# One written order from the end of attention to the cross softmax, PSUM banks handed back one by one

## The chip, the cores and the metric

The kernel runs on one core of one Trainium2 chip. The time is device microseconds of one execution. The engines are named as in the profile: PE (TensorE, the matmuls) with its weight loads PEld, DVE (VectorE), ACT (ScalarE), POOL (GpSimd) and SP (SyncE, here the queue that issues DMAs). PE writes to PSUM, which has eight banks of 128 x 512 f32; everything else lies in SBUF.

## The reference

One decoder layer over x (8 sequences of 128 tokens, width 512) and a context of the same shape, each of three parts added to x and followed by a layer norm:

```python
x = _layernorm(x + attn(x))        # 32 heads on 8 key heads, 4-bit weights, rope, causal softmax
x = _layernorm(x + xattn(x, ctx))  # 16 heads of 32
x = _layernorm(x + ffn(x))         # gated low-rank experts
```

The cross attention has an unusual softmax: it runs over the *batch and heads* (axis 0 of the scores), not over the keys:

```python
scores = jnp.einsum('bqd,bkd->bqk', Q, K) / sqrt(32)      # b = 8 sequences x 16 heads
attn = jax.nn.softmax(scores, axis=0)
```

So for each pair of positions there are 128 scores to be normalised together, and no cross output can be formed before the scores of all sequences and heads are there.

## The kernel before, in words

**Order.** From the first projection on, the instructions of PE, DVE, ACT and POOL are in an order written out by hand: each engine runs its instructions in the order in which the program issues them (`tc.manual_schedule(engines=ORDERED)`, line 700), and waits for data, for a free buffer or a free bank where it has to. `later(n, f)` (line 236) puts an operation off by n slots, and `tick()` issues what has come due.

**Attention** is a loop of 64 steps (line 745), eight sequences for each of the eight key heads; each step issues the letters of `SEQUENCE`. After every fourth step, 16 output units are queued (`attention_out`, line 436): the product of the attention result with the output weights, four column blocks c by four heads r. A unit "O" is two matmuls into the bank of one of two lanes (`out0`, `out1`); between heads the partial sum in the bank is multiplied by a ratio of scales, and after the fourth head it is added to `accT`. A unit therefore waits for the rescaling of the unit before it in its lane. The rescaling is made by ACT (line 456), or by DVE while the flag `ending` is set (line 454), which is from step 58 to step 63.

**The end of attention** (line 826, `ATT_END`) issues the last 16 O, mixed with 14 units "K" of the context's keys (three matmuls each, four to a bank, `x_projection`) and eight "X" (`turn_out`, line 816): four transposes of `accT`, the residual added to `acc` by DVE, and the layer norm's statistics by DVE, its power by POOL (line 222). The norm is applied later, by two ACT instructions, `nmr` and the scaling (lines 227 and 228). Then the pools of attention are closed, in SBUF and in PSUM.

**The cross softmax** (line 845 on). The query weights are loaded in four pieces and each is split into a high part (ACT, line 176) and a low part (POOL, line 177). `turn_x1` (line 881) transposes a normed sequence; ACT copies it as the high part and DVE makes the low part. `queries(r)` makes one block of queries, with 12 matmuls (line 679). `products(r)` makes the scores of group r (32 small matmuls into four banks, line 930). There are eight groups of 16 (sequence, head) pairs. A round of the loop at line 992 is: `exponentials(r)`, in which DVE subtracts the running maximum from each bank (line 954) and ACT takes the exponential; `products(r + 1)`; `queries(r + 3)`; `group_maximum(r + 1)`, five DVE instructions (lines 943 to 948); some of the 32 units of the context's values (`work`, the list `fill`); `group_sum(r)` on POOL (line 962). After the last round a sum over everything is made by PE with the identity (line 1042), then DVE's reciprocal (line 1089). All eight banks turn in a circle under one name here.

**The cross values and the FFN** (line 1324 on). For each sequence: `cross_values` (PE, line 1254), the residual, statistics, norm (`normalised` again, for the tokens "x" and for the gates "g"), transposes, the gate's and the main products. The first sequence's iteration also issues the last four value units.

Of the kernel before, what the change touches and what calls it, by code (L numbers as in the profile page):

```python
# [19 lines left out]
P = 128  # L20
# [22 lines left out]
ATT_END = 'OOKXOOKXOOKXOOKXOOKOOKOOKOOKKXKXKXKXKK'  # L43
# [9 lines left out]
FIRST_FILL = 4  # L53
ROUND_FILL = (0, 4, 4, 0, 4, 4, 4)
SUM_FILL = 4
# [65 lines left out]
BANKS_FIRST = {"turn": 6, "out0": 1, "out1": 1}  # L121
BANKS_SECOND = {"turn": 8}
BANKS = {m: 1 for m in ("pa", "pb", "pc", "pd", "sc", "tr", "av", "po")}
# [7 lines left out]
def decoder_kernel(ctx: ExitStack, tc: tile.TileContext, a: dict, out: bass.AP):  # L131
# [4 lines left out]

    psum = {"n": BANKS_FIRST, "turn": 0, "cm": tc.tile_pool(name="banks", bufs=1, space=PSUM)}
    psum["pool"] = psum["cm"].__enter__()

    def bank(tag, name, shape=(P, 512)):  # L140
        if tag == "proj" and "pa" in psum["n"]:
            tag = "p" + "abcd"[psum["turn"] % 4]
            psum["turn"] += 1
        tag = tag if tag in psum["n"] else "turn"
        return psum["pool"].tile(list(shape), F32, tag=tag, name=name, bufs=psum["n"][tag])
# [68 lines left out]
    def normalised(x, name):  # L214

        st = stat.tile([P, 6], F32, tag="bn", name=f"bn_{name}")
        nc.vector.bn_stats(st[:], x)
        mv = stat.tile([P, 2], F32, tag="mv", name=f"mv_{name}")
        nc.vector.bn_aggr(mv[:], st[:])
        rstd = stat.tile([P, 1], F32, tag="rstd", name=f"rstd_{name}")  # L220
        nc.vector.tensor_scalar(rstd[:], mv[:, 1:2], EPS, None, ALU.add)
        nc.gpsimd.tensor_tensor(rstd[:], rstd[:], minus_half[:], ALU.pow)
        nmr = stat.tile([P, 1], F32, tag="nmr", name=f"nmr_{name}")
        nc.vector.tensor_scalar(mv[:, 0:1], mv[:, 0:1], -1.0, None, ALU.mult)

        def apply():
            nc.scalar.activation(nmr[:], mv[:, 0:1], AF.Copy, scale=rstd[:])
            nc.scalar.activation(x, x, AF.Identity, scale=rstd[:], bias=nmr[:])

        return apply  # L230
# [34 lines left out]

    att_cm, att = pool("att")
# [95 lines left out]
    def projections(g, hf, w):  # L362

        n = f"{g}_{hf}"
        q = att.tile([P, REP, HN], F32, tag="q", name=f"q{n}", bufs=2)
# [48 lines left out]
    def attention_values(g, b, t, pt):  # L414
# [3 lines left out]
        if j == 0:  # L418
            for m in "hl":
                t["c" + m] = att.tile([P, REP, HN], F32R, tag="c" + m, name=f"c{m}{n}", bufs=2)  # L420
# [49 lines left out]
    def new_o(g):  # L470
# [6 lines left out]
        att.tile([P, KT, HN], F32, tag=tag, name=f"xraw{hf}", bufs=2) for hf, tag in enumerate(("q", "wo"))  # L477
# [13 lines left out]
    w0_q = att.tile([P, REP, D], F32R, tag="ch", name="w0_q", bufs=2)  # L491
# [87 lines left out]
    def open_keys():  # L579
# [4 lines left out]
        raw = xk["ctx0"] = att.tile([P, KT, HN], F32, tag="q", name="ctxraw0", bufs=2)  # L584
        nc.sync.dma_start(raw[:], a["ctxT"].rearrange("(k p) n -> p k n", p=P)[:, :, ts(0, HN)])

    def open_cross():
# [47 lines left out]
        def vals(t, tag="proj"):  # L635
# [4 lines left out]
            def part(kt):  # L640
                if kt == 0:
                    bk.append(bank(tag, f"pxv{t}"))
# [4 lines left out]
                if kt == KT - 1:  # L647
                    nc.tensor.matmul(bk[0][:], both[:], bias[:], start=False, stop=True)
                    nc.scalar.copy(values_of(t), bk[0][:])

# [12 lines left out]
    def values_of(t):  # L663

        hf, j = divmod(t, HALF)
        if len(xk["v"]) == hf:
            pl, tag = ((e2, "v"), (xk["work"], "ch0"))[hf]
# [3 lines left out]
    def x_projection(dst, m, w, x, hf, o, tag="proj"):  # L671
        bk = []

        def part(kt):
            if kt == 0:
                bk.append(bank(tag, f"px{m}{hf}_{o}"))
# [9 lines left out]
            if kt == KT - 1:  # L686
                nc.scalar.activation(dst(), bk[0][:], AF.Identity, bias=xb[m][:, o : o + 1])

# [50 lines left out]
    steps = NKV * B  # L739

# [4 lines left out]
    for s in range(steps):  # L745
# [23 lines left out]
        if s == steps - 4:  # L769
            stage("v", att, "wo")  # L770
        if s == steps - 3:
            for i in range(B):
                nc.sync.dma_start(acc[:, i, :], a["x"][i])
        if not units and s >= steps - 5:
# [39 lines left out]
        if b % HALF == HALF - 1:  # L814
            outs += attention_out(g, b // HALF, t)
    def turn_out(b):
# [5 lines left out]
        return lambda: normalised(acc[:, b, :], f"a{b}")  # L822

    ending[0] = False
    ends, last = [0], []
    for what in ATT_END:
        tick()
        if what == "O":
            outs.pop(0)()
        elif what == "K":  # L830
            late.pop(0)()
        else:
            stat_of = turn_out(ends[0])
            later(D_STAT, lambda f=stat_of: later(D_APPLY, f()))
            ends[0] += 1
    assert not outs and not late
    flush()
    close(xk["wcm"])
    close(att_cm)
    close(psum["cm"])  # L840
    psum.update(n=BANKS_SECOND, cm=tc.tile_pool(name="banks2", bufs=1, space=PSUM))
    psum["pool"] = psum["cm"].__enter__()


    e2_cm, e2 = pool("e2")
    xq_cm, xq = pool("xq")
    e_cm, ep = pool("e", "right")
    x1 = [
        {m: p.tile([P, KT, HN], F32R, tag=f"x1{m}", name=f"x1{m}{hf}") for m in "hl"}
        for hf, p in enumerate((e2, xq))  # L850
    ]
    qT = accT
    wq = {m: xq.tile([P, KT, D], F32R, name=f"xwq{m}") for m in "hl"}

    wq_splits = []
    gmax = ep.tile([P, GROUPS, S], F32, name="gmax")
    gsum = ep.tile([P, GROUPS - 1, S], F32, name="gsum")
    factor = ep.tile([P, 2, S], F32, name="factor")

    quads = {  # L860
        k: ep.tile([P, 4, HALF, S], F32, tag=f"E{k}", name=f"E{k}") for k in (1, 2, 3)
    }
    ep.tile([P, HALF, S], F32, tag="part", name="no_part", bufs=1)
    wq_raw = ep.tile([P, KT, D], F32, tag="E0", name="xwqraw")

    def load_wq(kt):
        raw = wq_raw[:, (kt + 1) % KT, :]
        nc.sync.dma_start(raw, a["WqT"][ts(kt, P), :])
        wq_splits.append(lambda: split(wq["h"][:, kt, :], wq["l"][:, kt, :], raw, nc.gpsimd))

    for kt in range(KT - 1):
        load_wq(kt)
        wq_splits.pop(0)()
    load_wq(KT - 1)
# [6 lines left out]
    def turn_x1(t):  # L881
        tr = transposed(bank("tr", f"tr_x1{t}", (P, KT, S)), t)
        hf, c = t // HALF, ts(t % HALF, S)
        hi, lo = (x1[hf][m][:, :, c] for m in "hl")
        nc.scalar.copy(hi, tr[:])
        return lambda: nc.vector.tensor_tensor(lo, tr[:], f32(hi), ALU.subtract)
# [14 lines left out]
    def scores_of(c):  # L901

        k = c // 4
        if k not in quads:
            memory = {4: (e2, "x1h"), 5: (e2, "x1l"), 6: (xk["kv"], "kT0")}
            if k == 7:
                quads[k] = qT[:, :, ts(0, HN)].rearrange("p c (j s) -> p c j s", j=HALF)
            elif k in memory:
                pl, tag = memory[k]
                quads[k] = pl.tile([P, 4, HALF, S], F32, tag=tag, name=f"E{k}")  # L910
# [27 lines left out]
    def group_maximum(r):  # L938
        top = xq.tile([P, HALF, S], F32, tag="top", name=f"top{r}", bufs=1)
# [10 lines left out]
    def exponentials(r, which=range(4)):  # L950

        for i in which:
            e = scores_of(4 * r + i)
            nc.vector.tensor_tensor(e, burst.pop(4 * r + i)[:], across(gmax[:, r, :]), ALU.subtract)  # L954
# [13 lines left out]
    def work(n=1):  # L968

        for _ in range(n):  # L970
            fill.pop(0)()


    for t in range(B):
        fill += xk["vals"](t)
    lows = [turn_x1(t) for t in range(HALF)]
    wq_splits.pop(0)()
    lows += [turn_x1(t) for t in range(HALF, HALF + 2)]
    for f in lows:
        f()  # L980
    queries(0)
    for f in [turn_x1(t) for t in range(HALF + 2, B)]:
        f()
    queries(1)
    products(0)
    queries(2)
    group_maximum(0)
    work(FIRST_FILL)


    early, lsum = slice(0, EARLY - 1), []
    for r in range(GROUPS - 1):
        exponentials(r)
        products(r + 1)
        if r + 3 < GROUPS:
            queries(r + 3)
        group_maximum(r + 1)
        work(ROUND_FILL[r])
        if r == EARLY - 1:
# [572 lines left out]
```

## Time and profile before

| | |
|---|---|
| time of three runs | 679.08, 681.67, 681.93 us (median 681.67) |
| the profiled execution | 679.53 us, of it span 677.7 us |
| busy in the span | PE 638.1 (94%), PEld 485.8 (72%), DVE 510.2 (75%), ACT 479.5 (71%), POOL 443.9 (65%) |
| mean granted PE clock | 0.991 |
| the tail of attention begins on PE (first O of `ATT_END`) | 488.44 us |
| last matmul of the key units starts on PE | 510.56 us |
| first query on PE | 519.51 us |
| first scores' maximum on DVE | 530.70 us |
| first / eighth group's exponentials begin on DVE | 534.96 / 581.48 us |
| last sum ends, reciprocal begins | 588.04 us |
| first cross values on PE | 591.87 us |

A line of the busy table gives, for a stretch of the span, its length, then busy microseconds and number of instructions of PE, PEld, DVE, ACT and POOL, the granted PE clock, the DMA engines' busy share and GB/s. A line of the timeline gives start, length, engine, line, operation, output and inputs, and in square brackets how long the engine was idle before it and who ended that. The chain is the work that ended last, followed back; each line has start, length, engine, tile and line.

### The profile page before, as it was taken

The numbers are of one execution on the slowest core, as the hardware profiler recorded it, in microseconds if no ns is written. First come the engines' busy times: TensorE is split into PE (matmuls) and PEld (weight loads), VectorE is DVE, ScalarE is ACT, GpSimd is POOL, SyncE is SP. The second block draws the span as 40 slices with busy tenths as digits, with TensorE's granted clock in tenths as the row PEclk, the third lists the DMA queues.
The fourth block names the chain that finished last, engine by engine and source line by source line (L and its number), as shares of the span: only waits on it lengthen the run. The fifth ranks groups of instructions, "written<-read, shape, count | busy, mean of one in ns | idle before, by whom it ended". The sixth has DMA issues, their size and how long they took to land.

```text
span 677.7 us, 11398 instructions
## 1 busy us (share of the span) xinstructions
PE 638.1 (94%) x3464; PEld 485.8 (72%) x3464; DVE 510.2 (75%) x1345; ACT 479.5 (71%) x1217; POOL 443.9 (65%) x416
## 2 busy tenths in 40 slices
PE   6899899999999999999999999989996999889996
PEld 4687677778778777787877778766774777666552
DVE  4978676778878788787877878777765699986565
ACT  3477888988898887888889887886465354345433
POOL 4654977979789797797977978876214279522104
PEclk9999999999999999999999999999998999899999
DMA  8664432343334234343331432326001000300003
GB/s 292 181 181 119 104 92 71 100 110 80 98 103 99 76 100 102 78 107 96 95 80 38 109 111 45 94 84 243 0 1 63 0 2 1 97 3 1 1 0 124
DMA packets 31775, 57.36 MB, mean 85 GB/s; under 512 B 4831, under 2 KB 7135, under 8 KB 31714
## 3 DMA queue, kind: packets, MB, share of 16 engines
q1 hardware_dynamic: 31714, 56.64, 31.0%
q8 instruction: 27, 0.44, 0.3%
q14 instruction: 34, 0.28, 0.1%
HBM read 33.55 MB, written 2.10 MB: 53 GB/s over the span
## 4 chain that ended last, share of the span: by engine, by line
PE 73%; DVE 12%; ACT 5%; POOL 5%; issue 3%; DMA 1%; SPq 0%; POOLq 0%; DVEq 0%; ACTq 0%
PE ps L311 22%; PE po L447 15%; PE sc L378 7%; PE av L417 7%; PE ps L297 4%; PE tr L409 4%; PE pf L1132 3%; DVE E L954 2%; DVE top L943 2%; PE pxk L679 2%; PE pxq L679 2%; POOL q L346 1%; DVE gmax L948 1%; PE trv L357 1%; PE pg L1119 1%
## 5 line engine op out<-in xcount | busy, mean ns | idle before, releaser
L311 PE MATMUL ps<-xh,w 128*128 128x512 f32 x336 | 157.3, 468 | 0.0
L321 DVE SCALAR_TENSOR_TENSOR part<-ps,scales,part 128x512 f32<-128x512 f32 x168 | 125.6, 748 | 29.0 <-ACT part L317 19.1
L456 ACT ACTIVATE po<-po,ratios 128x512 f32<-128x512 f32 x174 | 112.4, 660 | 44.3 <-PE po L447 39.8
L311 PE MATMUL ps<-xl,w 128*128 128x512 f32 x336 | 132.6, 395 | 0.0
L447 PE MATMUL po<-ch,wo 128*128 128x512 f32 x256 | 112.6, 440 | 5.0 <-DVE po L454 2.6
L344 POOL TENSOR_TENSOR t<-x,tables 128x512 f32<-128x512 f32 x70 | 90.3, 1290 | 40.7 <-DVE x L321 36.4
L345 POOL TENSOR_TENSOR sw<-sw,tables 128x512 f32<-128x512 f32 x71 | 92.0, 1296 | 19.9 <-DMA sw<-x 19.1
L392 ACT ACTIVATE p<-p,nmx 128x128 f32<-128x128 f32 x256 | 99.1, 391 | 4.8 <-DVE nmx L383 4.8
L447 PE MATMUL po<-cl,wo 128*128 128x512 f32 x256 | 100.9, 394 | 0.0
L346 POOL TENSOR_TENSOR q<-t,sw 128x512 f32<-128x512 f32 x62 | 81.8, 1320 | 12.8 <-DVE sw L345 8.4
L311 PEld LDWEIGHTS ps<-xl,w 128*128 128x128 f32 x336 | 63.7, 190 | 18.6 <-issue 10.1
L311 PEld LDWEIGHTS ps<-xh,w 128*128 128x128 f32 x336 | 63.5, 189 | 18.6 <-DVE nmx L383 6.3
L399 POOL TENSOR_TENSOR p<-p,rden 128x512 f32<-128x512 f32 x64 | 67.6, 1056 | 13.6 <-DVE rden L398 13.6
L378 PEld LDWEIGHTS sc<-k,q 128*128 128x128 f32 x512 | 67.4, 191 | 8.7 <-POOL q L346 3.1
L378 PE MATMUL sc<-k,q 128*128 128x128 f32 x512 | 68.6, 276 | 2.6 <-POOL q L346 2.6
L447 PEld LDWEIGHTS po<-ch,wo 128*128 128x128 f32 x256 | 48.1, 188 | 26.3 <-ACT po L456 7.3
L417 PE MATMUL av<-pt,v 128*128 128x512 f32 x128 | 65.5, 592 | 0.0
L321 DVE SCALAR_TENSOR_TENSOR x<-ps,scales,part 128x512 f32<-128x512 f32 x70 | 52.4, 749 | 14.7 <-PE ps L311 6.1
L383 DVE CUSTOM_DVE_ANT_0 p<-sc,causal 128x128 f32<-128x128 f32 x256 | 58.5, 285 | 6.1 <-PE sc L378 6.0
L317 ACT ACTIVATE part<-ps,scales 128x512 f32<-128x512 f32 x84 | 57.9, 689 | 0.0
L447 PEld LDWEIGHTS po<-cl,wo 128*128 128x128 f32 x256 | 48.4, 189 | 12.8 <-issue 4.5
L181 DVE TENSOR_TENSOR cl<-av,ch 128x512 fp32r<-128x512 f32 x64 | 44.1, 689 | 13.4 <-ACT ch L180 13.1
(253 smaller groups left out, 1264.5 us busy)
## 6 DMA issues: line engine op xcount, KB each, us to landing
sw<-x SPq DMA_DIRECT2D x160, 128.0 KB, 2.3
raw<-in_qkv SPq DMA_DIRECT2D x28, 384.0 KB, 3.2
oraw<-in_qw_o SPq DMA_DIRECT2D x32, 256.0 KB, 2.7
xraw<-in_xT SPq DMA_DIRECT2D x4, 512.0 KB, 6.6
ctxraw<-in_ctxT SPq DMA_DIRECT2D x2, 1024.0 KB, 5.0
acc<-in_x SPq DMA_DIRECT2D x8, 256.0 KB, 5.7
out<-o SPq DMA_DIRECT2D x8, 256.0 KB, 2.0
xwrawk<-in_WkT SPq DMA_DIRECT2D x1, 1024.0 KB, 5.5
```

The source lines that it names most:

```text
L311: nc.tensor.matmul(ps[:], w[:, kt, ts(j, HD)], x[:, kt, ts(hf, HN)], start=(i == 0), stop=(i == 1))
L321: nc.vector.scalar_tensor_tensor(to, ps[:], sc, parts[0][:], ALU.mult, ALU.add)
L344: later(delay("cos"), lambda: engine("cos").tensor_tensor(seqs(t[:]), seqs(x[:]), table(cos_t[m]), ALU.mult), True)
L345: later(delay("sin"), lambda: engine("sin").tensor_tensor(seqs(sw[:]), seqs(sw[:]), table(sin_t[m]), ALU.mult), True)
L346: later(delay("q"), lambda: engine("q").tensor_tensor(dst, t[:], sw[:], ALU.add), True)
L378: nc.tensor.matmul(sc[:, r, :], t["q"][:, r, ts(j, S)], t["k"][:, ts(j, S)], start=True, stop=True)
L383: nc.vector.tensor_tensor_reduce(out=p[:, r, :], in0=sc[:, r, :], in1=causal[:], scale=-1.0, scalar=3e38, op0=ALU.add, op1=ALU.min, accum_ ...
L392: nc.scalar.activation(p[:, r, :], p[:, r, :], AF.Exp, scale=-1.0, bias=nmx[:, r : r + 1], accum_out=den[:, r : r + 1],)
L399: nc.gpsimd.tensor_tensor(p[:], p[:], rden[:].unsqueeze(2).to_broadcast([P, REP, S]), ALU.mult)
L417: nc.tensor.matmul(av[:], t["v"][:, j, :], pt[:], start=True, stop=True)
L447: nc.tensor.matmul(ps[:], o_w[g][:, r, ts(c, P)], t["c" + m][:, r, :], start=(r == 0 and i == 0), stop=(i == 1), skip_group_check=True,)
L456: later(delay("out"), lambda: nc.scalar.activation(ps[:], ps[:], AF.Copy, scale=sc))
```

## The change

- **One order.** `ATT_END`, the code after it and the loop of rounds are replaced by a string, `ORDER`, with a letter for each unit: O, K, X as before; A applies a norm of X; T transposes a token sequence and L makes its low part; Q a block of queries; B products; M a group's maximum; E exponentials; S a group's sum; V a value unit; Z the last sum. All 32 V are in it.
- The flag `ending` is not cleared any more after step 63.
- X issues its statistics, the power and `nmr` at once; A is a single ACT instruction. `nmr` (minus mean times rstd) is made by POOL in one instruction instead of by DVE and ACT. This holds for all uses of `normalised`: 24 norms.
- **Banks.** One PSUM pool for the whole kernel. In the stretch of `ORDER` a free bank is taken from the front of a list, and `give` appends it to the list at the point of the program where its last reader is issued. The two lanes join the list after the last O.
- **Memory.** The query weights' raw pieces are loaded in step 60 and split in steps 62 and 63; they lie in the ring of attention's queries (`query_pool`). The first tokens, then two of the exponentials' tiles, then the FFN weights lie in the ring of attention's contexts (`context_pool`). The rest of the exponentials' memory is opened at the first E, where the key weights and the rest of attention's memory are closed.

```diff
-ATT_END = 'OOKXOOKXOOKXOOKXOOKOOKOOKOOKKXKXKXKXKK'
-FIRST_FILL = 4
-ROUND_FILL = (0, 4, 4, 0, 4, 4, 4)
-SUM_FILL = 4
+ORDER = (
+    'XOOXXOOXAKOKAKOOTTKAOOKAKOOTKLLOOLTKLOKOOQXXXKAKBMKXKQQK' 'EAVBAVVMVEQBTATMVVLVVVVVTTELLVLB'
+    'MVVQVEBVSMQVEVBVVSMQEVBMVVSQEVBVSVVSVVMSSEVVZV'
+)
...
+        elif tag in LANES:
+            tag = LANES[tag]
+        elif psum["ready"] is not None:
+            tag = psum["ready"].pop(0)
...
+    def give(*tiles):
+        for t in tiles:
+            tag = psum["tags"][id(t)][0]
+            psum["held"].discard(tag)
+            if psum["ready"] is not None:
+                psum["ready"].append(tag)
...
-        nc.vector.tensor_scalar(mv[:, 0:1], mv[:, 0:1], -1.0, None, ALU.mult)
-
-        def apply():
-            nc.scalar.activation(nmr[:], mv[:, 0:1], AF.Copy, scale=rstd[:])
-            nc.scalar.activation(x, x, AF.Identity, scale=rstd[:], bias=nmr[:])
-
-        return apply
+        nc.gpsimd.tensor_scalar(nmr[:], mv[:, 0:1], rstd[:], -1.0, ALU.mult, ALU.mult)
+        return lambda: nc.scalar.activation(x, x, AF.Identity, scale=rstd[:], bias=nmr[:])
...
+    def load_wq(kt):
+        raw = xk["raws"].tile([P, D], F32, tag="raw", name=f"xwqraw{kt}", bufs=3)
+        wq_raws.append(raw)
+        nc.sync.dma_start(raw[:], a["WqT"][ts(kt, P), :])
+        wq_splits.append(lambda: split(wq["h"][:, kt, :], wq["l"][:, kt, :], raw[:], nc.gpsimd))
...
         if s == steps - 4:
             stage("v", att, "wo")
+            xk["qcm"], xk["raws"] = pool("xr", "right")
+            for kt in range(KT - 1):
+                load_wq(kt)
...
+        if s >= steps - 2:
+            for i in range(2):
+                wq_splits.pop(0)()
+                if len(wq_raws) < KT:
+                    load_wq(KT - 1)
...
     def turn_out(b):
...
-        return lambda: normalised(acc[:, b, :], f"a{b}")
-
-    ending[0] = False
...
+        give(tr)
+        return normalised(acc[:, b, :], f"a{b}")
...
+    for what in ORDER:
+        n = count_of[what] = count_of.get(what, -1) + 1
+        tick()
+        if what == "O":
+            outs.pop(0)()
+            if not outs:
+                flush()
+                psum["ready"] += LANES.values()
...
+        elif what == "E":
+            if n == 0:
+                open_exponentials()
+            if n < GROUPS - 1:
+                exponentials(n)
+            else:
+                last_terms = last_exponentials()
...
-    fw = fwp.tile([P, KT, D], F32, name="fw")
+    fw = context_pool.tile([P, KT, D], F32, tag="ch", name="fw", bufs=2)
```

## The prediction

> **What bounds the kernel now.** I read the page's busy slices, then the busy time by stretches of 10 us, then the chain and the timeline inside 488 to 606 us, where the change lies.
>
> ```profile
> 500.00:510.00 10.00, 9.11 (x46) 6.85 (x46) 4.54 (x10) 5.21 (x10) 0.82 (x2) 1.00 0.00 0
> 510.00:520.00 10.00, 4.26 (x30) 3.32 (x28) 5.49 (x17) 8.86 (x18) 5.13 (x6) 0.97 0.33 105
> 520.00:530.00 10.00, 9.75 (x48) 7.53 (x51) 3.03 (x5) 3.05 (x6) 1.48 (x2) 0.69 0.01 2
> 530.00:540.00 10.00, 10.00 (x94) 8.08 (x88) 8.38 (x12) 3.67 (x7) 1.39 (x2) 1.00 0.00 0
> 540.00:550.00 10.00, 9.26 (x87) 7.05 (x90) 9.45 (x14) 4.87 (x9) 8.75 (x9) 1.00 0.01 2
> ```
>
> The columns are PE, PEld, DVE, ACT, POOL, clock, DMA. Between attention and the cross softmax PE idles (4.26 of 10) and then runs at 0.69 of its clock, while DVE is nearly free (3.03). From 540 on DVE is the full one. The timeline names the reason and the two starts that matter:
>
> ```profile
> 519.51 0.77 PE L679 MATMUL pxq<-x1h,xwqh 128*128 128x512 f32 x1 [4.84 <-POOL xwql L177]
> 530.70 0.69 DVE L947 COPY top<-xsc 128x512 f32<-128x512 f32 x1 [2.38 <-PE xsc L930]
> 534.96 2.48 DVE L954 TENSOR_TENSOR E<-xsc,gmax 128x512 f32<-128x512 f32 x4
> ```
>
> The first query waits 4.84 us for query weights that are fetched and split only after attention. From 534.96 the chain stays on DVE round after round:
>
> ```profile
> 541.91 2.48 DVE E L954 x4
> 544.39 0.61 DVE top L945
> ...
> 547.40 1.10 DVE gmax L948
> 548.50 0.02 issue
> 548.52 2.48 DVE E L954 x4
> ...
> 582.95 5.06 PE lsum L1042 x28
> ```
>
> A round lasts 548.52 - 541.91 = 6.61 us, without a gap; the eighth starts at 581.48. So the end of this stage is set by when DVE starts the first exponential step (E0), and by what else is put on DVE between the rounds. PE's idle time counts only as far as it moves E0.
>
> **The change part by part.** Unit costs, start to start, from the timeline. PE: two out matmuls (O) 0.46; a key unit (K) 0.69; four transposes (X, T) 0.44; a query (Q) 2.76; products (B) 1.11; a value unit (V) 0.69, 0.37 more at every fourth. DVE: X 1.74 (residual add 0.70, bn_stats 0.70, two small ones); the rescaling of a partial sum 0.70; the last of a lane 0.68; x1 low part (L) 0.62; M0 4.18, later maxima 4.13; E 2.50.
>
> *The tail of attention.* Time 0 is the tail's first instruction on PE, 488.44 before. The old tail rescaled on ACT (L456); the flag that says so is no longer cleared, so the 12 rescalings (8.4 us) go to DVE behind the statistics. Following ORDER with both engines in order: DVE does X0 0.6 to 2.3, O1, O2 to 3.7, X1, X2 to 7.2, O3, O4 to 8.6, X3 to 10.4, O5, O6 to 11.8. PE has O1 to O4, four X and a K by 5.4, and waits for O3's rescaling until 7.9 to issue O5, and after two K for O5's until 11.1 to issue O7. Then they alternate: DVE O7 12.4, O8 14.3 (PE had T, T, K before it), O9 15.0, O10 16.7 (two K), O11 17.4, L0, L1 18.6, O12, O13 20.0, L2, L3 21.2, O14 21.9, O15, O16 23.3. PE ends O16 at 22.4, Q0 at 25.2, X4 to X6 at 26.5, two K 27.9, B0 29.0, K, X7, K 30.8, Q1, Q2 36.4, the last K 37.0. DVE: X4 to X6 25.7 to 30.9, M0 35.1, X7 36.8. E0's tile lies in memory that the key weights held, so it waits for the last K: 37.1. PE's work to there is 31.7 us; it waits 5.4, DVE being the bound. Behind each waiting O on PE stand the key units, tokens and queries, all of which DVE or ACT wants next, so I count these waits in full; the longest, 2.5 us, is the first. DVE itself is idle 5 us of the 37: 1.3 before O8, 0.9 before O10, 2.4 before X4 (Q0 stands ahead of it on PE).
>
> *Query weights.* Three loads join SP's queue in step 60 ahead of the eight residual loads (one transfer of this size took 4.0 us to land; the residual is needed 25 us later: no cost). The fourth waits in step 62 for a free raw buffer, and nothing is behind it on SP. Two splits each in steps 62 and 63: on POOL 1.28 us each, idle from 479 to 493; without that cover the four cost 5.1. On ACT two casts of 0.62 come ahead of the bias rows at 477.32; of their 1.24 the 0.40 that ACT idled at 476.84 is free. The bias rows hold DVE L611, behind which an out product is rescaled, for which PE already waits at 481.23. So +0.9 on the tail's start (bounds 0 and 1.2).
>
> E0: 488.4 + 0.9 + 37.1 = 526.4 against 534.96, **8.5 us** earlier.
>
> *The rounds.* L4 to L7, before E0 now, go between the rounds: 4 x 0.62 = +2.5. Banks: B(r+1)'s last bank is the first that E(r) reads, so B starts 0.6 into E and takes 1.11, ready 0.75 before DVE wants it; a round without L4 to L7 stays 6.61. The moved V units make PE's work from E0 to the end of the last sum 25 (V) + 7.8 (B) + 13.8 (five Q) + 1.8 (T) + 4.5 (sums) = 53 us, against DVE's 20 + 29 + 2.5 + about 4 at the end = 55: PE is just covered, and each microsecond beyond that would be one at the end. POOL's group sum (5.1 of 6.6 a round) is covered; without that, +1.5 at the last. Eighth E: **6.0** earlier. The FFN weights load sooner, with no one waiting at either time; they would matter only after 586.5, where POOL waits for them now.
>
> *The last sum.* PE idled 2.25 us before it and its first part ran at clock 0.50 to 0.61 (584 to 588); it ended 2.0 us after its last term (585.97). In the new order two V stand just before it. Warm, it ends before DVE's other work (587.2, L1077), so the reciprocal comes 0.8 earlier (bounds 0, 0.8).
>
> *Values moved out of the cross values.* Today 12 value matmuls fill PE at 592.9 to 596.4, beside the residual's chain, which they don't set; gone, they return nothing. PE now idles about 3 us between the last V and xav. A row for that: after 2.25 us idle (580.7 to 582.95) the clock was 0.50 for about 3.3 us. Against it, two microseconds at 0.30 and 0.45 busy (459 to 461) left it at 1.00. At half clock, xav's last part, tr_av and tr_x (0.4 + 0.5 + 0.7) double: 1.6. I take +1.0 (bounds 0, 2).
>
> The Trainium skill, "TensorE: Matmul & The Clock Gate", Part 1, says that the clock halves after an idle window of about 3.4 us. The row above has it halve after less. By that rule the term would be 0 and the sum 1.0 lower; I keep the row.
>
> *The norm's -mean x rstd from ACT to POOL*, in 24 norms:
>
> ```profile
> 609.15 0.27 ACT L1120 COPY tmp_hT<-pg 128x128 f32<-128x128 f32 x1 [2.99 <-PE pg L1119]
> 609.31 0.30 ACT L227 ACTIVATE nmr_x<-mv_x,rstd_x 128x1 f32<-128x1 f32 x1
> 609.64 0.81 ACT L228 ACTIVATE acc<-acc,nmr_x,rstd_x 128x512 f32<-128x512 f32 x1
> 610.51 0.66 PE L878 MATMUL tr_x<-ident,acc 128*128 128x128 f32 x4 [0.39 <-ACT acc L228]
> ```
> ```profile
> L1410 POOL TENSOR_SCALAR nmr<-mv_f,rstd_f x6: 264/264/266, 663.1 to 671.5; 128x1 f32<-128x1 f32 x6
> ```
>
> In four tokens (609, 616, 623, 639) ACT's nmr is on the chain, with POOL's power done a microsecond earlier; POOL's 0.26 is hidden and 0.31 each goes, within PE's wait of 0.39: -1.2. Tokens 0, 1 and 7 wait for POOL itself: 0.36 on ACT and 0.07 on DVE against 0.31 there, or 0.7 if POOL is slowed as its power is (0.92 to 0.99 beside DVE, else 0.55). Taken +0.1. Sum -1.1 (bounds -1.9, +1).
>
> **Sum:** -6.0 - 0.8 + 1.0 - 1.1 = **-6.9**. The profiled execution took 679.53 (span 677.7): 672.6. The median of the three runs is 681.67, 2.1 above it: **674.8**. No change is within 0.5% (3.4 us), about what measurement can tell: 678.3 to 685.1.
>
> **Rivals.** *Gaps between rounds* (15%): the 0.75 us that B is ahead of DVE shrinks if the query's copy stands behind four exponentials on ACT (2.2 us), and each of seven rounds waits 0.3 to 0.6: +2 to +4, 677 to 679. For it: PE waits on banks in almost every round. Against: queries are made a round or more ahead.
>
> *More than that* (17%): no ACT delay (-0.9), no slow clock (-1.0), DVE waiting less in the tail, where my walk leaves it 5 us idle of 37: -2 to -5, 670 to 673.
>
> *Slower* (10%): DVE's queue in the tail. Each O waits for a rescaling behind statistics, and nothing can pass it. The price is E0: at +6.9 (0.43 at each of the 16 O, E0 at 533.3) all is lost; the measurable loss begins at 0.65 each, and at 0.8 each the time is 688. For it: PE waited 0.57 and 0.75 us on rescalings at 500 and 503 even with ACT, which had less to do, making them. Against: DVE follows PE in 0.05 to 0.2 us wherever it waits.
>
> *The change does nothing* (5%): the memory of E0 or of the tokens is freed by something later than I see, and E0 stays within 2 us of 535: 680 to 683. For it: three stages' tiles now lie in rings of attention's, so each waits for that ring's last reader. Against: those readers (the last O, Q3, Q7) stand ahead in PE's own order.
>
> **How the numbers follow.** My forecast (53%): 673 to 677. Faster by over 0.5%: 53 + 17 + about half of the gaps 7 = 77, less 3 for what is unseen: 0.74. Within: the other gaps, no effect, the unseen: 0.15. Slower: 0.11. The range: 669.5 to 682 leaves the slow rival and a few of the fast ends out.
>
> **What would show it.** E0 at 525 to 528; Q0 starting near 512 without a wait for xwql; clock 1.00 there; rescalings on DVE with PE waiting twice at the tail's start, 2 to 3 us each; rounds of 6.6 with three L-stretched ones; the eighth E near 575.5; xav at slow clock; no nmr on ACT. Wrong if E0 is after 530, or a round is over 7.5.

## The result, and the profile after

The changed kernel takes 687.83 us (median of four, 685.91 to 688.11) against 680.38 us of the kernel before beside it: 1.0103 times as long, 95% interval 1.0068 to 1.0138. So it is slower by some 7 us, where 6.9 us less was forecast. The profiled execution took 687.6 us, its span is 685.8 us (before 677.7), and the mean granted clock 0.98 (before 0.991).

The stretches after, with the columns of those before (PE, PEld, DVE, ACT, POOL, clock, DMA):

```profile
500.00:510.00 10.00, 7.28 (x26) 5.37 (x27) 8.51 (x18) 2.21 (x3) 3.10 (x8) 0.83 0.01 2
510.00:520.00 10.00, 9.46 (x49) 7.48 (x47) 8.03 (x14) 4.34 (x7) 0.00 (x0) 1.00 0.00 0
520.00:530.00 10.00, 9.94 (x78) 8.20 (x79) 6.89 (x16) 2.19 (x3) 1.94 (x5) 1.00 0.01 2
...
580.00:590.00 10.00, 7.96 (x41) 6.15 (x37) 7.74 (x11) 5.68 (x10) 4.75 (x4) 0.86 0.42 150
590.00:600.00 10.00, 7.82 (x69) 5.34 (x67) 7.77 (x16) 0.78 (x2) 5.15 (x20) 0.84 0.01 2
600.00:610.00 10.00, 6.44 (x49) 4.92 (x50) 6.75 (x13) 2.26 (x4) 2.27 (x2) 0.50 0.00 0
```

The hole that the change was to close is closed: from 510 to 520 PE is busy 9.46 (before 4.26), from 520 to 530 the clock is 1.00 (before 0.69). But new weak places stand in the table: 500 to 510 (PE 7.28 at clock 0.83; before 9.11 at 1.00), 590 to 600 (7.82 at 0.84; before 8.41 at 1.00), and 600 to 610, all of it at half clock, where the kernel before has:

```profile
600.00:610.00 10.00, 8.81 (x96) 6.11 (x96) 8.71 (x27) 3.95 (x10) 2.56 (x3) 1.00 0.01 3
```

The stretch from 580 to 590 was no better before (PE 7.75 at 0.83).

The marks of the stage on the timeline after. They are the first query (without a wait now), the first maximum, the first and the eighth group's exponentials, and the reciprocal:

```profile
520.63 0.40 PE L704 MATMUL pxq<-x1h,xwqh 128*128 128x512 f32 x1
529.49 0.69 DVE L972 COPY group_top<-xsc 128x512 f32<-128x512 f32 x1
535.58 2.48 DVE L980 TENSOR_TENSOR E<-xsc,gmax 128x512 f32<-128x512 f32 x4
...
584.55 1.29 DVE L980 TENSOR_TENSOR accT<-xsc,gmax 128x512 f32<-128x512 f32 x2
...
594.63 0.94 DVE L1138 RECIPROCAL gmax<-lsum 128x128 f32<-128x128 f32 x1
```

E0, the first group's exponentials, starts at 535.58, later after the span's start than before (534.96). To see which stretch lost what, I cut both spans at the same events. Attention's end is the last of the 64 reciprocals `rden` on DVE, at 475.48 before and 481.16 after. The last column is one of the two fastest experiments below, in which four losses are mended.

| stretch | before | after | difference | forecast | four mends (e9_slots) |
|---|---|---|---|---|---|
| span's start to attention's last reciprocal | 475.48 | 481.16 | +5.68 | 0 | +0.02 |
| to the tail's first instruction on PE | 12.96 | 16.00 | +3.04 | +0.9 | 0.00 |
| to E0 | 46.52 | 38.42 | -8.10 | -9.4 | -8.19 |
| to the eighth E | 46.52 | 48.97 | +2.45 | +2.5 | +2.46 |
| to the last reciprocal | 6.56 | 10.08 | +3.52 | -0.8 | -0.60 |
| to the span's end | 89.66 | 91.17 | +1.51 | -0.1 | +0.31 |
| sum | 677.7 | 685.8 | +8.1 | -6.9 | -6.0 |

The gain that was forecast is there, in the third row. It is eaten by four others: the first, second, fifth and sixth.

**Second row.** At the end of attention DVE makes the bias rows of the values (three small instructions). The three before, and then the timelines of DVE, POOL and PE after:

```profile
478.16 1.06 DVE L611 TENSOR_TENSOR bv_raw<-bv_raw,bv_rows 2x512 f32<-2x512 f32 x1 [0.16 <-ACT bv_rows L610]
479.26 0.47 DVE L612 TENSOR_SCALAR bv_rows<-bv_rows,ident 2x512 fp32r<-2x512 f32 x1
479.77 0.74 DVE L613 SCALAR_TENSOR_TENSOR bv_rows<-bv_raw,ident,bv_rows 2x512 fp32r<-2x512 f32 x1
```

```profile
482.92 0.76 DVE L477 TENSOR_SCALAR po<-po,ratios 128x512 f32<-128x512 f32 x1
484.39 1.75 DVE L635 TENSOR_TENSOR bv_raw<-bv_raw,bv_rows 2x512 f32<-2x512 f32 x1 [0.71 <-ACT bv_rows L634]
486.18 1.38 DVE L636 TENSOR_SCALAR bv_rows<-bv_rows,ident 2x512 fp32r<-2x512 f32 x1
487.59 1.63 DVE L637 SCALAR_TENSOR_TENSOR bv_rows<-bv_raw,ident,bv_rows 2x512 fp32r<-2x512 f32 x1
489.15 1.40 DVE L477 TENSOR_SCALAR po<-po,ratios 128x512 f32<-128x512 f32 x2
```
```profile
484.32 4.37 POOL L201 TENSOR_TENSOR xwql<-xwqraw,xwqh 128x512 fp32r<-128x512 f32 x3
```
```profile
489.95 0.50 PE L470 MATMUL po<-ch,wo 128*128 128x512 f32 x1 [3.17 <-DVE po L477]
```

The three took 1.06, 0.47 and 0.74 us before, 4.76 us instead of 2.27 now, and DVE waits 0.71 us instead of 0.16 for ACT's row, which now stands behind two casts of the query weights: 2.49 and 0.55 us, together the 3.04. POOL makes the low parts of the query weights at the same time. Behind them on DVE stands the rescaling for which PE waits 3.17 us.

**Fifth row.** ACT, POOL and DVE at the end of the cross softmax:

```profile
583.79 0.59 ACT L673 COPY xv<-pxv 128x512 f32<-128x512 f32 x1 [2.21 <-PE pxv L672]
584.28 0.74 ACT L1071 ACTIVATE gmax<-gmax 128x640 f32<-128x640 f32 x1
```
```profile
585.10 1.54 POOL L1073 TENSOR_TENSOR gsum<-gsum,gmax 128x640 f32<-128x640 f32 x1 [6.04 <-ACT gmax L1071]
586.60 1.45 POOL L989 TENSOR_TENSOR part<-E 128x512 f32<-128x512 f32 x1
588.13 2.62 POOL L989 TENSOR_TENSOR part<-part,E 128x512 f32<-128x512 f32 x2
```
```profile
592.13 0.43 DVE L1011 TENSOR_TENSOR halved<-accT 128x256 f32<-128x256 f32 x1 [4.01 <-POOL gsum L991]
```

POOL idles 6.04 us for a small exponential on ACT (`gmax`, of the early groups' maxima), which is issued late and stands behind a copy that waits 2.21 us for PE's value unit. Then POOL makes the sum of group 6, and DVE's `halved`, which takes the same buffer ("part"), waits 4.01 us for it.

**Sixth row.** The chain through the first cross token:

```profile
603.26 0.17 DVE rstd_x L245
603.43 0.07 issue
603.50 0.94 POOL rstd_x L246
604.44 0.09 issue
604.53 1.35 POOL nmr_x L248
605.88 0.03 issue
605.91 0.82 ACT acc L249
```

POOL's `nmr` takes 1.35 us on the chain, and 1.26 at the second token, while DVE weights exponentials beside it; in the six tokens after that it takes 0.26 to 0.30. Token 1's transposes come 18.85 us after the reciprocal, before 15.45.

### The profile page after: what moved, and what is told of

Read it like the earlier page. It is cut to its first block, busy times and chain, and to the rows that moved or that the text cites. A ratio compares the mean times of both kernels' runs of the same rounds, so it can differ in the third digit from the quotient of the medians.

```text
span 685.8 us, 11391 instructions
## 1 busy us (share of the span) xinstructions
PE 641.4 (94%) x3464; PEld 486.7 (71%) x3464; DVE 519.2 (76%) x1333; ACT 467.0 (68%) x1181; POOL 451.7 (66%) x440
## 4 chain that ended last, share of the span: by engine, by line
PE 69%; POOL 11%; DVE 8%; ACT 4%; issue 4%; DMA 3%; SPq 0%; POOLq 0%; DVEq 0%; ACTq 0%
PE ps L334 18%; PE po L470 13%; PE sc L401 7%; PE av L440 6%; PE pxq L704 3%; POOL sw L368 3%; PE pf L1180 3%; PE ps L320 3%; PE tr L432 3%; PE pxv L668 3%; PE pxk L704 2%; DMA sw<-x 2%; POOL t L367 2%; POOL q L369 2%; POOL p L422 1%
## 5 line engine op out<-in xcount | busy, mean ns | idle before, releaser
L479 ACT ACTIVATE po<-po,ratios 128x512 f32<-128x512 f32 x162 | 105.0, 661 | 39.8 <-PE po L470 35.3
L205 DVE TENSOR_TENSOR cl<-av,ch 128x512 fp32r<-128x512 f32 x64 | 44.1, 688 | 13.7 <-ACT ch L204 13.4
```

Of the source, the lines that this page charges most:

```text
L479: later(delay("out"), lambda: nc.scalar.activation(ps[:], ps[:], AF.Copy, scale=sc))
```

## The experiments

The kernel before was timed again beside each batch: 679.7 us beside the first four kernels, 678.97 beside the next four, 680.07 beside the last three. All ratios are to it.

**Attention's banks in strict turn, in the old kernel** (e1_turn). In the first stage the old pool gives its six banks out of one ring of six; the changed kernel takes them as b0, b1, ... b5, b0. That is the only thing that the change does to the first 60 of the 64 steps, besides the pools of memory. The edit to the old kernel:

```diff
-BANKS_FIRST = {"turn": 6, "out0": 1, "out1": 1}
+BANKS_FIRST = {**{f"b{i}": 1 for i in range(6)}, "out0": 1, "out1": 1}
...
+        if "b0" in psum["n"] and tag not in psum["n"]:
+            tag = f"b{psum['six'] % 6}"
+            psum["six"] += 1
```

> Before, with one thing of the change alone: in attention the six banks are named and taken in a strict turn (b0 to b5), instead of from one ring of six from which the pool chooses; nothing else differs, and everything after attention is as before. It tells where the 5.7 us come from by which the changed kernel is late already at the last step of attention (481.16 against 475.48), in code whose instructions the change does not touch. Theory A, the bank order: the waits on PE differ (56 transposes wait for DVE instead of 43, 44 values matmuls for DVE and ACT instead of 15), so the time is 3.5 to 6 us above before, and the last reciprocal of attention comes at 479 to 481. Theory B, luck of one execution (DMA landings at the start): no change, within 1.5 us of before, and the last reciprocal between 474 and 478.

Measured: 682.78 us, ratio 1.0041 (1.0027 to 1.0055): +2.8 us, less than the 3.5 to 6 that I expected of the bank order. The last reciprocal of attention comes at 479.53. So the order of the banks costs something in attention, about half of the +5.68.

**Attention's memory split into pools, in the old kernel** (e2_pools).

```diff
-        q = att.tile([P, REP, HN], F32, tag="q", name=f"q{n}", bufs=2)
+        q = query_pool.tile([P, REP, HN], F32, tag="q", name=f"q{n}", bufs=2)
...
-                t["c" + m] = att.tile([P, REP, HN], F32R, tag="c" + m, name=f"c{m}{n}", bufs=2)
+                t["c" + m] = context_pool.tile([P, REP, HN], F32R, tag="c" + m, name=f"c{m}{n}", bufs=2)
```

> Before, with another thing of the change alone: attention's queries and contexts lie in two SBUF pools of their own, so that the addresses of all of attention's tiles are those of the changed kernel; engines, order and waits are as before. Theory C, the addresses (slower DMA landings or port conflicts) make attention 3.5 to 6 us longer: 684 to 686. Theories A and B: no change, within 1.5 us. Its profile also serves as a second one of attention as it was before.

Measured: 679.97 us, ratio 1.0003 (0.9989 to 1.0017); the last reciprocal at 475.73. These pools have no part in it.

**The group sums earlier** (e3_sum, from the changed kernel): the sums of groups 2 to 5 are issued together after M6, so that the small exponential and POOL's work of the end come a round earlier.

```diff
-    'MVVQVEBVSMQVEVBVVSMQEVBMVVSQEVBVSVVSVVMSSEVVZV'
+    'MVVQVEBVSMQVEVBVVSMQEVBMVVSSSSQEVBVVVVVMSEVVZV'
```

> The changed kernel, with the four group sums S2 to S5 issued together after the sixth maximum (M6) and so before the last two rounds' copies on ACT; no instruction more or less. In the changed kernel POOL idles 6.04 us before the product of the early sums, because ACT's exponential of the early maxima stands behind the copy of the seventh value tile, and DVE then idles 4.01 us. If that misplaced exponential is what lengthened the last sum (10.08 us from the eighth exponentials to the reciprocal, 6.56 before), it is 5.7 to 6.6 here and the time falls by 3.3 to 4.3 us below the changed kernel's. Rival: POOL's group sum itself is late (it ends at the same time), then less than 1 us.

Measured: 681.64 us, ratio 1.0027 (1.0011 to 1.0044), some 5 us under the changed kernel. In its profile POOL and DVE stand so:

```profile
576.44 1.56 POOL L1073 TENSOR_TENSOR gsum<-gsum,gmax 128x640 f32<-128x640 f32 x1
577.94 1.31 POOL L989 TENSOR_TENSOR part<-E 128x512 f32<-128x512 f32 x1
579.33 2.65 POOL L989 TENSOR_TENSOR part<-part,E 128x512 f32<-128x512 f32 x2
```
```profile
581.98 1.29 DVE L980 TENSOR_TENSOR accT<-xsc,gmax 128x512 f32<-128x512 f32 x2
...
587.97 0.96 DVE L1138 RECIPROCAL gmax<-lsum 128x128 f32<-128x128 f32 x1
```

POOL has no gap left before the product, and from the eighth E to the reciprocal it is 5.99 us instead of 10.08: 4.1 us, the fifth row. The rest of the difference lies in attention (in these two executions its last reciprocal is at 478.56 here, 481.16 there), whose program is the same; see the first point of the next section.

**Four value units back in the cross values** (e4_values, from the changed kernel).

```diff
-    'MVVQVEBVSMQVEVBVVSMQEVBMVVSQEVBVSVVSVVMSSEVVZV'
+    'MVVQVEBVSMQVEVBVVSMQEVBMVVSQEVBVSVVSVMSSEZ'
```

> The changed kernel, with the last four value units back in the first iteration of the cross values, as before the change. In the changed kernel PE runs at clock 0.50 from 597.7 to 611 and the first two tokens' chain is 3.3 us longer than before. Theory: PE's idle time before and between the first cross values, which those matmuls used to fill, lowers the clock; then the clock stays 1.00 there, the four transposes of the first two tokens take 0.5 instead of 1.1 and 0.9 us, and the time falls by 1 to 2 us. Rival: it is only POOL's nmr (1.34 and 1.25 us beside DVE's weighting); then less than 0.5 us.

Measured: 687.39 us, ratio 1.0106 (1.0083 to 1.0129): nothing is gained, where I expected 1 to 2 us and a clock of 1.00 at the first cross tokens. In its profile the clock is at half from about 2 to 9 us after the reciprocal although the units stand there, and the rest of the span is 92.6 us, in the changed kernel 91.2. (Its tail, too, has a spell of half clock that the changed kernel's has not.) The question comes again below with the other losses mended.

**Banks by order of release** (e5_ring: e3_sum, and in attention each bank handed back where its last reader is issued).

```diff
-    psum = {"turn": 0, "ready": None, "named": None, "held": set(), "tags": {}}
+    psum = {"turn": 0, "ready": [f"b{i}" for i in range(TURNING)], "named": None, "held": set(), "tags": {}}
...
         nc.scalar.copy(pt[:], tr[:])
+        give(tr)
```

> The changed kernel with the sums of groups 2 to 5 issued together (as in e3_sum, 1.0027 of before), and with attention's six banks given back in the order of their last readers instead of in strict turn. Theory (the strict turn is a loss of its own inside attention, +2.8 us when it was put into the old kernel alone): the last reciprocal of attention comes 2 to 3 us earlier than in e3_sum (478.56), near the old 475.5, and the time falls by as much, to about 0.9986 of before (0.997 to 1.000). Rival (the strict turn costs only in the old kernel's pools; the loss in the changed one comes of its other memory): the last reciprocal stays within 1 us of 478.6, the time at 1.0027.

Measured: 683.46 us, ratio 1.0049 (1.0031 to 1.0066); the last reciprocal at 477.98. My theory missed: no gain. But this order was not the old one either. Of PE's 2314 matmuls up to the tail some 225 still wait for another engine than in the old kernel (289 with the strict turn), so the run doesn't decide between "the order of banks" and "something else in the changed kernel". It is the base of the next three.

**The mean's product of two tokens off POOL** (e6_nmr: e5_ring, and cross tokens 0 and 1 as in the old kernel).

```diff
+        if on_act:
+            nc.vector.tensor_scalar(mv[:, 0:1], mv[:, 0:1], -1.0, None, ALU.mult)
+        else:
+            nc.gpsimd.tensor_scalar(nmr[:], mv[:, 0:1], rstd[:], -1.0, ALU.mult, ALU.mult)
...
+            if on_act:
+                nc.scalar.activation(nmr[:], mv[:, 0:1], AF.Copy, scale=rstd[:])
...
-        apply[i] = normalised(acc[:, i, :], f"x{i}")
+        apply[i] = normalised(acc[:, i, :], f"x{i}", i < 2)
```

> e5_ring with the mean's product of the norms of cross tokens 0 and 1 back on DVE and ACT; the other norms keep it on POOL. Theory (POOL is slowed while DVE weights beside it: 1.34 and 1.25 us for an operation of 0.27 us, pow to apply 2.41 and 1.93 us against 1.37 and 0.96): about 2.0 us faster than e5_ring (1.0 to 2.2), token 1's transposes that much earlier after the reciprocal. Rival (the loss in the first cross tokens is TensorE's half clock alone, from 597.7 to 611 in the changed kernel): within 0.6 us of e5_ring.

Measured: 680.73 us, ratio 1.0012 (0.9998 to 1.0026), 2.7 us under e5_ring. Token 1's transposes come 16.81 us after the reciprocal, against 18.63 in e5_ring: 1.8 earlier, and the rest of the span is 1.5 us shorter (89.66 against 91.13). The other part of the 2.7 us is not of this edit in the two profiles: the tail starts 16.01 us after attention's last reciprocal here and 17.63 in e5_ring, by a spell of half clock (see e7_bias). The rival, half clock alone, is out as the whole cause; of the changed kernel's 3.40 us at token 1's transposes the edit explains 1.8.

**The query weights split after the bias rows** (e7_bias: e5_ring, with the four splits as orders W in the tail).

```diff
-        if s >= steps - 2:
-            for i in range(2):
-                wq_splits.pop(0)()
...
-    'XOOXXOOXAKOKAKOOTTKAOOKAKOOTKLLOOLTKLOKOOQXXXKAKBMKXKQQK' 'EAVBAVVMVEQBTATMVVLVVVVVTTELLVLB'
+    'WXWOOWXXOOXAKWOKAKOOTTKAOOKAKOOTKLLOOLTKLOKOOQXXXKAKBMKXKQQK' 'EAVBAVVMVEQBTATMVVLVVVVVTTELLVLB'
...
+        elif what == "W":
+            split_wq()
```

> e5_ring with the four splits of the query weights moved from attention's last two steps into the tail's first orders, so that POOL has none of them while DVE makes the bias rows. Theory (the three bias-row operations took 4.76 us instead of 2.27 because POOL ran beside them, and TensorE waited 3.2 us for DVE behind them): the three fall to about 2.3 us, the tail's first transposes come 1.5 to 2.5 us earlier relative to attention's last reciprocal, and the first exponentials and the time as much, to about 2.1 us under e5_ring (1.0 to 2.5). Rival (DVE's walk through the tail takes the gain up, or the splits now slow the tail's own norms on POOL): first exponentials within 0.7 us of e5_ring's, time too.

Measured: 679.0 us, ratio 0.9988 (0.9972 to 1.0004), 4.5 us under e5_ring. DVE's rows at the same place:

```profile
480.83 1.06 DVE L648 TENSOR_TENSOR bv_raw<-bv_raw,bv_rows 2x512 f32<-2x512 f32 x1 [0.17 <-ACT bv_rows L647]
481.93 0.47 DVE L649 TENSOR_SCALAR bv_rows<-bv_rows,ident 2x512 fp32r<-2x512 f32 x1
482.44 0.74 DVE L650 SCALAR_TENSOR_TENSOR bv_rows<-bv_raw,ident,bv_rows 2x512 fp32r<-2x512 f32 x1
```

They have the old kernel's durations to a hundredth of a microsecond, PE's wait of 3.2 us is gone, and the tail starts 12.97 us after attention's last reciprocal (before 12.96, changed kernel 16.00). From there to E0 it is 38.45 us, as in the changed kernel, so DVE's walk took nothing of it back. That is 3.0 us, more than the 1.0 to 2.5 that I expected, because the edit also takes ACT's two casts from before the bias rows (0.17 us of waiting for ACT again): 2.49 and 0.55 us. The run doesn't part the two; the rows do. In e5_ring's profile the tail starts 17.63 us after the last reciprocal: its clock fell to 0.50 behind the very wait that is gone here, and that is the other 1.6 of the 4.5 us, if the executions that were not profiled did the same.

**All four mends** (e8_all: e5_ring with both edits above).

> All four mends together: sums of groups 2 to 5 early, banks by order of release, the mean's product of cross tokens 0 and 1 on DVE and ACT, query weights split in the tail. If the four losses are each their own and add: e5_ring less 2.0 less 2.1, about 0.9926 of before (0.990 to 0.996), so faster than both kernels. Rival (they share one wait, so that the second mend finds nothing left): no more than 1 us under the better of e6_nmr and e7_bias.

Measured: 676.41 us, ratio 0.9944 (0.9924 to 0.9964). The two gains add (2.7 and 4.5 us under e5_ring alone, 7.05 together), and the kernel is faster than both the kernel before and the changed one.

**The old order of banks, exactly** (e9_slots: e8_all without the release order in attention, but with the old kernel's sequence of 623 bank numbers; e10_slots_alone: that sequence alone in the changed kernel). In e9_slots the instructions of PE, DVE, ACT and POOL up to the tail are the old kernel's, and PE waits for the same engines (all but 9 of the 2314 matmuls, counted as for e5_ring; the expectation below counts rows in another way).

```diff
+        elif psum["turn"] < len(SLOTS):
+            tag = f"b{SLOTS[psum['turn']]}"
+            psum["turn"] += 1
```

> e8_all, but attention's banks taken in exactly the order in which the old kernel took them (its sequence of 623 bank numbers written out), so that TensorE's instructions and their waits up to the tail are the old kernel's one by one; in e5_ring to e8_all some 350 of the first 1740 rows still waited for something else. Theory (order of banks): attention's last reciprocal returns to 475.5 to 476.2 (477.8 in e8_all), the time falls by about 2.4 us, to 0.991 of before (0.989 to 0.993). Rival (something else of the changed kernel, its memory or its loads, delays attention's middle): the last reciprocal stays at 477.5 or later and the time at 0.9944.

> The changed kernel with the old kernel's order of banks in attention, and nothing else mended. Theory (order of banks, +2.8 us in the old kernel): 1.0062 of before (1.004 to 1.008; the changed kernel was at 1.0103), the last reciprocal at 475.5 to 476.5. Rival (order of banks is nothing to this kernel): 1.009 to 1.011.

Measured: e9_slots 673.76 us, ratio 0.9915 (0.9894 to 0.9935), last reciprocal of attention 475.50; e10_slots_alone 684.1 us, ratio 1.0063 (1.0042 to 1.0084), last reciprocal 477.36. Both times are where the theory put them, though each interval overlaps the one that it is to be told from. The last reciprocal of e10_slots_alone is later than the 475.5 to 476.5 that I expected; but its ninth is late already, at 91.17 (e9_slots 89.53), with the same instructions up to there. So I count from the ninth reciprocal to the 64th, in all thirteen traces:

| banks in attention | kernels | us |
|---|---|---|
| the old sequence | before, e2, e9, e10, e11 | 386.31, 386.50, 385.97, 386.19, 386.62 |
| strict turn | e1, changed, e3, e4 | 387.82, 388.50, 388.28, 388.17 |
| by release | e5, e6, e7, e8 | 387.23, 388.43, 388.96, 388.13 |

Every value of the other rows is above all of the old sequence's. The place is steps 31 to 36: 35.2 to 35.7 us in the old sequence, 35.9 to 37.8 in the others. What is late there begins a few steps earlier, where POOL waits for a transfer that swaps the halves of a query for the rope: 1.0 us in the five kernels with the old sequence, 2.1 to 3.0 in the eight others. POOL in the changed kernel, PE's rows that follow from it, and then the same of e9_slots:

```profile
237.72 1.28 POOL L367 TENSOR_TENSOR t<-x,tables 128x512 f32<-128x512 f32 x1
241.65 1.28 POOL L368 TENSOR_TENSOR sw<-sw,tables 128x512 f32<-128x512 f32 x1 [2.65 <-DMA sw<-x]
```
```profile
257.91 0.71 PE L401 MATMUL sc<-k,q 128*128 128x128 f32 x4 [1.34 <-POOL q L369]
```
```profile
234.59 1.28 POOL L385 TENSOR_TENSOR t<-x,tables 128x512 f32<-128x512 f32 x1
236.90 1.29 POOL L386 TENSOR_TENSOR sw<-sw,tables 128x512 f32<-128x512 f32 x1 [1.03 <-DMA sw<-x]
...
252.89 1.41 PE L419 MATMUL sc<-k,q 128*128 128x128 f32 x8
```

POOL waits 1.6 us longer (the transfer lands 4.1 us after its issue, where the median is 2.3; in both kernels a load of weights is issued right behind it) and works without a pause from then on, and 16 us later PE waits 1.34 us for the query, and again 1.24 us at 287. PE's wait for queries between 250 and 290 is 2.6 us in the changed kernel, 1.7 in e1_turn, 1.6 in e8_all; with the old sequence it is 0.3 (before), 0.1 (e9_slots) and 0.4 (e10_slots_alone). Why the order of the banks makes that one transfer late was not found.

**Value units back, once more** (e11_values_back: e9_slots, and the last four units behind the reciprocal).

```diff
-    'MVVQVEBVSMQVEVBVVSMQEVBMVVSSSSQEVBVVVVVMSEVVZV'
+    'MVVQVEBVSMQVEVBVVSMQEVBMVVSSSSQEVBVVVVMSEZ'
```

> e9_slots with the last four groups of cross values after the reciprocal again, as in the old kernel. Theory (with nothing left to fill them, the first cross tokens run at half clock, for about 1.0 us): 0.5 to 1.2 us under e9_slots, token 1's transposes within 0.3 us of the old 15.46 after the reciprocal (16.5 in e8_all). Rival (the round without them leaves TensorE idle, and the clock falls there instead): same as e9_slots within 0.5 us, or slower.

Measured: 673.53 us, ratio 0.9909 (0.9889 to 0.9928), which can't be told from e9_slots; I expected 0.5 to 1.2 us less. PE's clock (the number after the bracket) in e9_slots, then in e11_values_back:

```profile
592.00:594.00 2.00, 1.18 (x6) 0.50 0.00 0
594.00:596.00 2.00, 2.00 (x9) 0.50 0.00 0
```
```profile
587.00:590.00 3.00, 2.86 (x28) 0.50 0.00 0
...
592.00:594.00 2.00, 2.00 (x33) 1.00 0.00 0
594.00:596.00 2.00, 1.29 (x20) 1.00 0.00 0
```

The clock is up from 590.4 on, but the spell just ahead of that, with the first cross values and the first of the units in it, is at half clock. Token 1's transposes come 16.41 us after the reciprocal: earlier than in e9_slots (17.09), no earlier than in e8_all (16.45), which has no units there, and not within 0.3 us of the old 15.45. The span after the reciprocal is 89.31 us, in e9_slots 89.97, but in e8_all 89.3 too. So the slow clock at the first cross tokens is real, and that the units mend it is not shown.

## Why the prediction was wrong, step by step

- **"Code before the tail is unchanged"** was never written down but it carried the sum: no term stood for attention. This step failed first. The diff shows it, in the function `bank`: the ring's choice became `turn % TURNING`. I told of that under "one PSUM pool" and priced it only for the cross softmax. It cost 2.8 us in the old kernel alone (e1_turn); behind the ninth reciprocal, what it lengthened there and here is PE's waits for queries (1.7 and 2.6 us against 0.3). Of the profiled +5.68, 2.19 lies behind the ninth reciprocal (388.50 against 386.31) and 3.49 ahead of it. Most of the latter is this one execution: with the same program up to there the ninth reciprocal came at 92.66 in the changed kernel, 90.28 in e3_sum and 90.55 in e4_values, against 89.17 before.
- **The query weights, +0.9 on the tail's start (bounds 0 and 1.2)**: +3.04, outside the bounds. I asked whether POOL was free (it was) and counted ACT's casts, which cost 0.55, but not what POOL does to DVE's instructions at its side, 2.49. e7_bias shows it: without the splits there the term is 0.0.
- **The walk, E0 at 37.1 after the tail's start**: 38.42. DVE bounds the tail as forecast, and PE's long wait came where the walk had it: 505.26, 8.1 us into the tail (forecast 7.9), 2.26 us long. Missed was the clock behind that wait, by a row that the prediction itself quoted (half clock after 2.25 us of idleness) and used only for the cross values. All ten traces with the new order have this wait, 2.26 to 2.27 us long. In eight the clock halved behind it and E0 came at 38.3 to 38.5; in e4_values and e8_all it stayed up and E0 came at 37.63. So 0.7 to 0.8 of the 1.3 is the clock's; where the other 0.5 went was not traced.
- **Rounds, +2.5 for L4 to L7, otherwise 6.61**: right, +2.45. Exponentials start 6.63, 7.07, 8.63, 6.61, 6.63, 6.81 and 6.59 us apart. The third round holds three of the four low parts and is over the 7.5 that I had set as a sign of being wrong; the sum is right all the same.
- **"POOL's group sum is covered; without that, +1.5"**: this failed. The price was taken from POOL's own work (5.1 us a round), not from the letters: in ORDER the sums of groups 2 to 5 come late, and the exponential that is issued with the last of them stands behind a value copy on ACT. It cost 4.1 us (e3_sum); mended, the last stretch is 5.99 us (forecast 5.75).
- **The last sum warm, -0.8**: not in the changed kernel, where the clock was at half from 587.2 to 590.6; with the group sums mended, -0.6 in e3_sum and e9_slots.
- **Half clock at the first cross tokens, +1.0 (bounds 0 and 2)**: the right kind and near the size. With the old `nmr` at tokens 0 and 1 and the clock at half, token 1's transposes come 1.0 to 1.6 us later than before (16.45 to 17.09 us after the reciprocal in e6_nmr, e8_all and e9_slots, against 15.45). No run parts the clock from what else differs there.
- **`nmr` on POOL, -1.1**: -0.31 a token came true: the transposes of tokens 1 to 4 follow one another 0.33 us closer than before (6.68 to 6.69 us against 7.01 to 7.02). But "+0.1, or 0.7 if POOL is slowed" for tokens 0, 1 and 7 should have taken the other end, and that was too small: 1.35 and 1.26 us instead of 0.27 at tokens 0 and 1, 1.8 us in all (e6_nmr).
- **The rivals**: the slow one that I gave (DVE's queue in the tail) was not what happened, nor were the gaps between rounds. Slower came from four small losses at once, two of which are, in the main, one thing: POOL and DVE beside each other.

With the four mends the sum is -6.0 in the profile and the ratio 0.9915, where -6.9 was forecast. The gain that I saw was real; what I had not costed was larger.

The Trainium skill, "SBUF — State Buffer", section "Who interferes with whom", states a rule that fits the second and sixth row: a VectorE instruction with two SBUF inputs contends with a GpSimd instruction that reads SBUF, and the later one waits for the whole of the other. The rows agree in kind: DVE's two instructions of that form went from 0.74 to 1.63 us and from 1.06 to 1.75, and POOL's `nmr` from 0.27 to 1.35. The bias rows' TENSOR_SCALAR, which has one tensor as input, was slowed too (0.47 to 1.38); the rescalings beside them, which read PSUM, stayed at 0.70 to 0.76.

## What to carry to other kernels

Before costing a reordering, look for what the diff changes *outside* the stretch it is about: here one line that picks a bank cost some 2 to 3 us in a loop whose instructions were the same. Before work goes to an idle POOL, see what DVE reads from SBUF at its side: here small instructions on the chain became 1.6 to 5 times as long. When helper work (a group sum) may slip to the end of a pipeline, find its last due time from the order of issue, with every queue that its inputs stand in, and not from how busy its engine is.

## What the hardware showed that I had not expected

- DVE's three instructions on two partitions took 1.06, 0.47 and 0.74 us in the kernel before, where only the first had a subtraction of POOL beside it for half its length, and 1.75, 1.38 and 1.63 beside POOL's 128x512 subtractions all along, while three of POOL's took 4.37 us instead of 3.79. POOL's product on 128x1 went from 0.27 to 1.35 beside DVE's 128x512 products.
- A wait of a fixed length does not fix the clock. After the same wait of 3.2 us ahead of the tail's start it stayed at 1.00 in the changed kernel and fell to 0.50 for 6.8 us in e4_values (first line the changed kernel, second e4_values, each from where PE goes on):

```profile
490.00:496.00 6.00, 6.00 (x27) 4.58 (x28) 3.83 (x6) 1.86 (x3) 0.35 (x1) 1.00 0.00 0
```
```profile
487.00:493.00 6.00, 5.49 (x15) 4.42 (x16) 3.22 (x5) 0.59 (x1) 0.97 (x1) 0.50 0.00 0
```

  That moved the tail by 2.7 us (18.71 after attention's last reciprocal, against 16.00). The spells of half clock after attention last 3.4, 6.8, 10.3 or 13.7 us, apart from the last one of each trace. So a wait of 2 to 3 us on PE should be priced with the risk of what such spells cost here, 0.7 to 2.7 us more.
- The order in which PSUM banks are taken, with instructions and data the same, moved the landing of a DMA transfer in the middle of attention (POOL waits 1.0 us for it in the five kernels with the old sequence, 2.1 to 3.0 in the eight others), and with it PE's waits for queries: 0 to 0.5 us at that place in the five, 0.7 to 1.5 in the eight.
